# Two attention sublayers of a decoder as one row of pipeline steps with shared buffers

## The chip, the cores and the metric

The kernel runs on one core of a Trainium2 chip. The metric is device time in microseconds (us) of one launch, the median of several runs. PE is TensorE (matmuls and transposes), DVE is VectorE, ACT is ScalarE, POOL is GpSimd, SP is SyncE, which here only issues DMAs.

## The reference

A decoder of four layers, post-layernorm, over 4096 tokens (64 sequences of 64) of width 256. Each layer has self-attention, a second mixer and a feed-forward part: twelve sublayers. The tenth and eleventh are the fourth layer's two attentions, the twelfth its feed-forward part with ternary weights.

```python
def _L3_attn_ref(x, Wq, Wk, Wv, Wproj, q_rms_w, k_rms_w, subln_w):
    H, D = (16, 128)
    q = (x @ Wq).reshape(B, T, H, D)
    k = (x @ Wk).reshape(B, T, H, D)
    v = (x @ Wv).reshape(B, T, H, D)
    q = rmsnorm(q, q_rms_w)
    k = rmsnorm(k, k_rms_w)
    scores = jnp.einsum('bthd,bshd->bhts', q, k) * scale + bias[None]   # bias: ALiBi
    scores = jnp.where(causal[None, None], scores, -jnp.inf)
    attn = jax.nn.softmax(scores, axis=-1)
    y = jnp.einsum('bhts,bshd->bhtd', attn, v)
    y = rmsnorm(y, subln_w)
    y = y.transpose(0, 2, 1, 3).reshape(B, T, H * D)
    return y @ Wproj
...
def _L3_xattn_ref(hidden_states, encoder_hidden_states, attention_mask, Wq, bq, Wk, bk, Wv, bv, Wo, qn_w, kn_w):
    # NH = 16 query heads, NKV = 4 key and value heads, HD = 128
    q = (hidden_states @ Wq + bq).reshape(b, s, NH, HD).transpose(0, 2, 1, 3)
    k = (encoder_hidden_states @ Wk + bk).reshape(b, se, NKV, HD).transpose(0, 2, 1, 3)
    v = (encoder_hidden_states @ Wv + bv).reshape(b, se, NKV, HD).transpose(0, 2, 1, 3)
    k = jnp.repeat(k, GROUPS, axis=1)
    v = jnp.repeat(v, GROUPS, axis=1)
    q = _rmsnorm(q, qn_w)
    k = _rmsnorm(k, kn_w)
    scores = jnp.einsum('bhsd,bhed->bhse', q, k) * scale
    scores = scores + attention_mask[:, None, :, :]
    probs = jax.nn.softmax(scores.astype(jnp.float32), axis=-1).astype(q.dtype)
    out = jnp.einsum('bhse,bhed->bhsd', probs, v)
    out = out.transpose(0, 2, 1, 3).reshape(b, s, NH * HD)
    return out @ Wo
...
x = _layernorm(x + _L3_attn_ref(x, ...), axis=-1)
x = _layernorm(x + _L3_xattn_ref(x, ctx_2048, mask_1xSxS2_ff0, ...), axis=-1)
x = _layernorm(x + _L3_ffn_ref(x, ...), axis=-1)
```

## The kernel before

**Tiling.** The 4096 tokens are 8 groups (g) of 4 tiles (t) of 128 tokens; a tile holds two sequences. Rows live in SBUF as X[g], the encoder's rows, already transposed, as CT[g]. In both sublayers the unit of work is a step (g, t, hb), where hb is one half of the 16 heads, so 64 steps each. A step's queries are two projections of 512 columns, u=0 and u=1, four heads each. The tenth sublayer also projects two times 512 columns of keys and of values in each step. The eleventh has only four key and value heads, so one projection of k and one of v serve both steps of a tile; they are made in the step with hb=0.

**Stages.** Both sublayers are software pipelines of four stages, one pass of a Python loop per step i: projections of step i, transposes and scores of step i−1, transposes of the probabilities and the products with the values of step i−2, the output projection of step i−3. All matmuls and transposes of a stage go through PE.

**The order.** Both loops stand under a manual schedule of PE: PE runs its instructions in the order of the Python code. The other engines' instructions are placed by a scheduler. A wait between engines is a semaphore; a buffer of a pool has a tag and a number of copies (bufs), and its next user waits for the readers of the one before. PSUM has the tags p (projections, two banks), tr (transposes, two banks), s (scores, one), y (products with the values, two) and acc (output, one).

The order of PE in a step of the eleventh sublayer is: transposes of both queries of step i−1 (qT0, qT1, `heads_transposed`, lines 1643 and 275), with hb=0 of step i−1 the transposed keys (kT), then with hb=0 of step i the projections k and v, then q0 and q1 (`projected`, L1966 the addition of the bias), then at the last tile of a group the transposes of the next group's rows (xt), then the transposed probabilities of step i−2 (pt), the scores of step i−1 (L2000), the output of step i−3 (L2047) and the products with the values of step i−2 (L2030). The softmax is L2006 to L2014: times the queries' norm, plus mask, maximum, minus maximum (DVE), exponential (ACT), sum, reciprocal (DVE), times reciprocal (POOL). PSUM is left by `copy` (L254 on ACT, L256 on DVE). Norms are a sum of squares (ACT, DVE) and a power on POOL (L269). z (L2053) is the residual sum, `layernorm` (L306 its last part) turns four tiles of z into the new rows.

The order of PE in a step of the tenth: v0 v1 of step i−2, then qT0 kT0, q0, qT1 kT1, q1, the transposed y of step i−3 (yt), k0, pt of i−2, scores of i−1, k1, output of i−3, values of i−2.

**Buffers.** Each sublayer has its own pool of working tiles and its own PSUM pool. The pool of the tenth hands its tiles over one by one, the eleventh's pool as a whole: its first tiles wait until the tenth's last use is over. Weights of 1 MB come from a ring of eight buffers by SP's queue (`load`, L366); `big_weight` loads two of them. The biases of k and v and the mask are tiles of the eleventh's pool, loaded at its start. To bring the two halves of a value tile to the other half of the partitions, two small DMAs on SP's queue write vs from v (L1788 in the tenth, L1979 in the eleventh). The weight of the tenth's output projection is scaled once on ACT by the learned weight of y's norm.

**Around it.** The twelfth sublayer's ternary weights are prepared inside the eleventh (`ternary`, L2098 to L2109), some of its rows in the last 12 steps (`l3_prepare`), and its own first tiles wait for the whole of the pools before.

Of the kernel before, what the change touches and what calls it, by code (L numbers as in the profile page):

```python
# [2 lines left out]

# [6 lines left out]
F32 = mybir.dt.float32  # L10
# [4 lines left out]
ALU = mybir.AluOpType  # L15
# [12 lines left out]
LAYERS = 7  # L28
# [206 lines left out]
class Decoder:  # L235
# [154 lines left out]
    def run(self, layers):  # L390
# [12 lines left out]
        for g in (1, 2):  # L403
# [5 lines left out]
            self.l2_l3, self.l3_xattn, self.l3_ffn,  # L409
# [959 lines left out]
    def l2_l3(self, ctx):  # L1369

        shared = self.pool(ctx, "l2s", 1)
        linear = Linear(self, shared)
        for body in (self.l2_mix, self.l3_attn):
            with ExitStack() as part:
                self.psum = self.pool(part, "psum_" + body.__name__, 2, space=PSUM, reuse_waits="tile")
                body(part, linear)
# [355 lines left out]
    def l3_attn(self, ctx, linear):  # L1734


# [5 lines left out]
        wk = ctx.enter_context(self.tc.tile_pool(name="l3a", bufs=2, reuse_waits="tile"))  # L1742
        wq, wkk, wp, wv = (self.big_weight(n) for n in ("l3a_wq", "l3a_wk", "l3a_wproj", "l3a_wv"))
# [5 lines left out]
        steps = [(g, t, hb) for g in range(self.n_groups) for t in range(TG) for hb in range(2)]  # L1749
# [34 lines left out]
        def value(i, u):  # L1784
            v = projected(i, wv, u, "v", 2)
            vs = wk.tile([P, 4, P], F32, tag="vs", name="vs")
            for b in range(2):
                nc.sync.dma_start(out=vs[half(b)], in_=v[half(1 - b)])  # L1788
            state[i, "v", u] = v, vs
# [84 lines left out]
        with self.tc.manual_schedule(engines={mybir.EngineType.PE}):  # L1874
            n = len(steps)
            bank = lambda name: self.bank(name, bufs=2)
            linear.first(wk, bank)
            bias = self.distances(wk)
            for w in wp:
                nc.scalar.activation(w, w, AF.Copy, scale=sw)  # L1880
            xts[0] = wk.tile([P, 2, NTOK], F32, tag="xt", name="xt")
            ahead = []
            for i in range(n + 3):
                first, second, third, fourth = i < n, 1 <= i <= n, 2 <= i <= n + 1, i >= 3
                if first and steps[i][1:] == (0, 0):
                    if steps[i][0] + 1 < self.n_groups:
                        ahead = linear.parts(steps[i][0] + 1, wk, bank)
                    zs[steps[i][0]] = wk.tile([P, TG, D], F32, tag="z", name="z", bufs=1)
                if first and steps[i][0] == 0 and steps[i][2] == 0:
                    t = steps[i][1]  # L1890
                    ps = self.transpose4([self.X[0][:, t, c * P : (c + 1) * P] for c in range(2)], "xt")
                    self.copy(xts[0][:, :, t * P : (t + 1) * P], ps[:, :D].rearrange("p (c n) -> p c n", c=2))
                if third:
                    value(i - 2, 0)
                    value(i - 2, 1)
                if second:
                    turn(i - 1, 0)
                if first:
                    query(i, 0)
                if second:  # L1900
                    turn(i - 1, 1)
                if first:
                    query(i, 1)
                if fourth:
                    outputs_turned(i - 3)
                if first:
                    key(i, 0)
                if third:
                    turned(i - 2)
                if second:  # L1910
                    scores(i - 1)
                if first:
                    key(i, 1)
                if fourth:
                    output(i - 3)
                if third:
                    values(i - 2)
                if first:
                    g, t, hb = steps[i]
                    if ahead:  # L1920
                        ahead.pop(0)()
                        if len(ahead) == 5:
                            ahead.pop(0)()
                    if (t, hb) == (TG - 1, 0) and g + 1 < self.n_groups:
                        xts[g + 1] = self.transposed(self.X[g + 1], wk, "xt")

    def l3_xattn(self, ctx):


# [5 lines left out]
        wk = self.pool(ctx, "l3x", 2)  # L1935
        wq = self.big_weight("l3x_wq")
        kv = self.weight("l3x_wkv").rearrange("p (i c n) -> p i c n", i=2, c=2)
        self.load(kv[:, 0], ins["l3x_wk"].rearrange("(c p) n -> p c n", p=P))
        self.load(kv[:, 1], ins["l3x_wv"].rearrange("(c p) n -> p c n", p=P))
        wo = self.big_weight("l3x_wo")  # L1940
        bq = self.weight("l3x_bq")
        bk, bv = (wk.tile([P, 512], F32, tag=name, name=name, bufs=1) for name in ("l3x_bk", "l3x_bv"))
        for t, name in ((bq, "l3x_bq"), (bk, "l3x_bk"), (bv, "l3x_bv")):
            self.load(t, ins[name].broadcast_to([P, t.shape[1]]))
        qw, kw = self.column("l3x_qw"), self.column("l3x_kw")
        both = wk.tile([P, 1], F32, tag="both", name="both", bufs=1)
        nc.vector.tensor_scalar(both, kw, qw, 1.0 / math.sqrt(P), ALU.mult, ALU.mult)
        mask = wk.tile([P, S], F32, tag="mask", name="mask", bufs=1)
        for b in range(2):
            self.load(mask[b * S : (b + 1) * S], ins["mask"])  # L1950
        half = lambda b: slice(b * S, (b + 1) * S)
        steps = [(g, t, hb) for g in range(self.n_groups) for t in range(TG) for hb in range(2)]
# [16 lines left out]
        def keys_values(g, t):  # L1969
            ct = self.CT[g]  # L1970
            cs = lambda c: ct[:, c, t * P : (t + 1) * P]
            k = projected(cs, lambda c, n: kv[:, 0, c, n], slice(0, 512), bk, "k", 1)
            r = self.small(4, "hrk")
            rms(k, r, "k")
            nc.gpsimd.tensor_tensor(k, k, r.unsqueeze(2).broadcast_to([P, 4, P]), ALU.mult)
            v = projected(cs, lambda c, n: kv[:, 1, c, n], slice(0, 512), bv, "v", 2)
            vs = wk.tile([P, 4, P], F32, tag="vs", name="vs")
            for b in range(2):
                nc.sync.dma_start(out=vs[half(b)], in_=v[half(1 - b)])  # L1979
            return k, v, vs  # L1980

        def queries(g, t, hb):
            xt = xts[g]
            qs = []
            r = self.small(8, "hrq")
            for u in range(2):
                cols = slice((2 * hb + u) * 512, (2 * hb + u + 1) * 512)
                q = projected(
                    lambda c: xt[:, c, t * P : (t + 1) * P], lambda c, n: wq[c][:, n], cols, bq[:, cols], "q", 4
                )  # L1990
                rms(q, r[:, 4 * u : 4 * u + 4], "q")
                qs.append(q)
            return qs, r

        def scores(g, t, hb, qT, r):
            kT = tiles[g, t][0]
# [18 lines left out]
            return s  # L2015

        def turned(s):
            ps = self.transpose4([s[:, 2 * j : 2 * j + 2, :].rearrange("p h k -> p (h k)") for j in range(4)], "pt")
            pt = wk.tile([P, 4, P], F32, tag="pt", name="pt")
            self.copy(pt.rearrange("p j q -> p (j q)"), ps)  # L2020
            return pt

        def values(g, t, hb, pt):
            _, v, vs = tiles[g, t]
# [10 lines left out]
            for h2 in range(2):  # L2035
                yt = wk.tile([P, 4, P], F32, tag="yt", name="yt", bufs=4)
                self.copy(yt.rearrange("p j q -> p (j q)"), pss[h2])
                yts.append(yt)
            return yts

        def output(g, t, hb, yts):
# [3 lines left out]
            for h in range(8):  # L2045
                n = 8 * hb + h
                nc.tensor.matmul(  # L2047
                    acc[:, :D], yts[h % 2][:, h // 2, :], wo[n // 8][:, (n % 8) * D : (n % 8 + 1) * D],
                    start=n == 0, stop=n == 15,
                )  # L2050
            if hb == 1:
                x, z = self.X[g], zs[g]
# [3 lines left out]

        ahead = []
        with self.tc.manual_schedule(engines={mybir.EngineType.PE}):
            n = len(steps)
            xts[0] = self.transposed(self.X[0], wk, "xt")  # L2060
            for i in range(n + 3):
                if 1 <= i <= n:
                    g, t, hb = steps[i - 1]
                    qs, r = state.pop((i - 1, "q"))
                    qT = [self.heads_transposed(wk, q, "qT", bufs=4) for q in qs]
                    if hb == 0:
                        tiles[g, t][0] = self.heads_transposed(wk, tiles[g, t][0], "kT", both)
                if i < n:
                    g, t, hb = steps[i]
                    if hb == 0:  # L2070
                        tiles[g, t] = [*keys_values(g, t)]
                        if t == 0:
# [243 lines left out]
```

## Time and profile before

| | us |
|---|---|
| median of 3 runs | 4425.86 (4423.49 to 4430.15) |
| profiled execution | 4426.47 |
| its span, first to last instruction | 4424.7 |
| tenth sublayer in the span | about 1924 to 3222 |
| eleventh sublayer | about 3222 to 4124 |
| twelfth sublayer | about 4124 to 4425 |

Granted TensorE clock over the span: 0.971 of full speed. The starts of the score products (L2000) give the length of the eleventh's steps: in the even part 14.15 us from a step with hb=1 to one with hb=0, and 12.34 us from one with hb=0 to the one with hb=1. Durations in this profile that the reader will meet again: a projection of 512 columns is 1.72 us of PE, four transposes 0.44, scores 1.08, output 3.55 to 3.65, values 1.09; on DVE an operation on 128x512 numbers is 0.68 us, the next begins 0.60 us after it, or 0.72 if it needs its result; on ACT 0.58 to 0.63; on POOL a product 1.04 and a power 1.01.

A row of the timeline is to be read as: start in us of the span, duration, engine, line of the kernel, operation, written tile <- read tiles, shape, number of equal instructions, and in brackets the engine's idle time before it with what ended it.

### The profile page before, as it was taken

The page shows a single profiled execution, that of the slowest core. Times are in us where ns is not written, and L with a number is a line of the kernel's source. Part 1 is how long each engine was busy: PE and PEld are TensorE (multiplying, and loading weights), DVE is VectorE, ACT ScalarE, POOL GpSimd, SP SyncE. Part 2 cuts the span into 40 slices and gives each one's busy share as a digit, 9 for nine tenths or more (in the row PEclk, how much of TensorE's full clock was granted, in tenths as well). Part 3 has the DMA queues.
Part 4 walks back from the last instruction along what each step waited for, and adds up shares of the span by engine and source line. Part 5 has one row for each costly group of instructions (what it writes and reads, how often), then busy time and mean ns, then how long its engine had stood idle before and what let it go on. Part 6 is the DMA issues. An engine that isn't in the chain of part 4 may idle for free. (4 is left out here: it accounts for less than half of the span.)

```text
span 4424.7 us, 73910 instructions
## 1 busy us (share of the span) xinstructions
PE 4091.3 (92%) x28788; PEld 2647.7 (60%) x28808; DVE 3092.2 (70%) x6239; ACT 2022.6 (46%) x3667; POOL 1475.5 (33%) x1501
## 2 busy tenths in 40 slices
PE   8889999989888999869999999999979999999898
PEld 6645566666665555436666666666646666666566
DVE  6744548888674677877777777777667776776676
ACT  5546545666424666534444444444323322233344
POOL 4411121322421111035555555555433333333111
PEclk9989998999999999979999999999989999999999
DMA  2100012333100000111111111111310000000000
GB/s 83 65 20 10 1 39 68 84 68 75 43 2 20 1 1 1 38 34 25 30 25 30 25 29 25 30 26 29 90 30 11 10 11 11 10 11 11 8 15 17
DMA packets 99685, 128.26 MB, mean 29 GB/s; under 512 B 14916, under 2 KB 72452, under 8 KB 97928
## 3 DMA queue, kind: packets, MB, share of 16 engines
q1 hardware_dynamic: 99336, 123.53, 11.1%
q8 instruction: 228, 3.74, 0.4%
q14 instruction: 121, 0.99, 0.1%
HBM read 61.87 MB, written 19.42 MB: 18 GB/s over the span
## 5 line engine op out<-in xcount | busy, mean ns | idle before, releaser
L269 POOL TENSOR_TENSOR hrq<-hrq,neg_half 128x4 f32<-128x4 f32 x256 | 270.7, 1058 | 510.3 <-DVE hrq L267 510.2
L269 POOL TENSOR_TENSOR rstd<-rstd,neg_half 128x4 f32<-128x4 f32 (+1 forms) x171 | 149.1, 873 | 716.8 <-DVE rstd L267 642.6
L1152 DVE TENSOR_REDUCE mc<-sq 128x2 f32<-128x512 f32 x512 | 317.0, 682 | 62.4 <-PE sk L1150 62.3
L1158 ACT ACTIVATE e<-sk 128x512 f32<-128x512 f32 x512 | 265.3, 609 | 110.0 <-PE sk L1150 109.8
L269 POOL TENSOR_TENSOR hrk<-hrk,neg_half 128x4 f32<-128x4 f32 x160 | 188.2, 1176 | 289.4 <-DVE hrk L267 279.3
L1147 PE MATMUL sq<-l1x 32*128 32x256 f32 x2048 | 273.8, 405 | 2.6 <-DVE mc L1152 1.6
L1657 PE MATMUL p<-l3a_wq,xt 128*128 128x512 f32 x512 | 244.5, 601 | 11.0 <-DVE v L256 9.9
L1657 PE MATMUL p<-l3x_wq,xt 128*128 128x512 f32 x512 | 238.0, 609 | 14.0 <-DVE k L1966 13.8
L1150 PE MATMUL sk<-l1x 32*128 32x256 f32 x2048 | 250.3, 390 | 0.0
L1657 PE MATMUL p<-l3a_wk,xt 128*128 128x512 f32 x512 | 247.2, 606 | 0.0
L1147 PEld LDWEIGHTS sq<-l1x 32*128 32x128 f32 x2048 | 207.4, 193 | 56.5 <-issue 23.9
L2047 PE MATMUL acc<-l3x_wo,yt 128*128 128x256 f32 x1024 | 238.0, 386 | 0.7 <-ACT yt L254 0.7
L1657 PE MATMUL p<-l3a_wv,xt 128*128 128x512 f32 x512 | 234.3, 600 | 0.4 <-ACT y L93 0.4
L1864 PE MATMUL acc<-l3a_wproj,yt 128*128 128x256 f32 x1024 | 232.3, 380 | 0.0
L1864 PEld LDWEIGHTS acc<-l3a_wproj,yt 128*128 128x128 f32 x1024 | 194.7, 191 | 53.0 <-issue 29.2
L2047 PEld LDWEIGHTS acc<-l3x_wo,yt 128*128 128x128 f32 x1024 | 189.3, 190 | 28.2 <-ACT yt L254 0.9
L1150 PEld LDWEIGHTS sk<-l1x 32*128 32x128 f32 x2048 | 187.0, 185 | 6.6 <-issue 2.9
L1958 ACT ACTIVATE sq<-q 128x512 f32<-128x512 f32 x128 | 80.7, 630 | 206.7 <-DVE q L1966 153.5
L1657 PEld LDWEIGHTS p<-l3x_wq,xt 128*128 128x128 f32 x512 | 97.4, 196 | 126.8 <-issue 116.2
L1848 POOL TENSOR_TENSOR hry<-hry,neg_half 128x8 f32<-128x8 f32 x64 | 106.2, 1659 | 193.4 <-DVE hry L1844 193.4
L275 PEld LDWEIGHTS qT<-ident,q 128*128 128x128 f32 x1024 | 118.8, 141 | 76.6 <-issue 63.8
L1186 PE MATMUL ret<-e,vt 128*32 128x256 f32 x2048 | 140.6, 390 | 18.1 <-DVE mc L1152 17.0
(395 smaller groups left out, 10207.3 us busy)
## 6 DMA issues: line engine op xcount, KB each, us to landing
vs<-v SPq DMA_DIRECT2D x320, 128.0 KB
x<-in_x SPq DMA_DIRECT2D x8, 512.0 KB
ct<-in_ctxT SPq DMA_DIRECT2D x8, 512.0 KB
cn<-in_ctx SPq DMA_DIRECT2D x8, 512.0 KB
l1x<-in_ctx SPq DMA_DIRECT2D x128, 32.0 KB
l1x_x<-x SPq DMA_DIRECT2D x8, 512.0 KB
l1x<-l1x_x SPq DMA_DIRECT2D x128, 32.0 KB
l1x_r<-r SPq DMA_DIRECT2D x128, 32.0 KB
```

Source lines behind the costliest of these rows:

```text
L269: nc.gpsimd.tensor_tensor(out, out, self.neg_half[:, :n], ALU.pow)
L275: self.nc.tensor.transpose(ps[:, j * P : (j + 1) * P], blk, self.ident)
L1147: nc.tensor.matmul(ps[:, n, :], x_[rows, j, part], c_[rows, j, :], start=True, stop=True)
L1150: nc.tensor.matmul(ps[:, n, :], c_[rows, j, part], x_[rows, j, :], start=True, stop=True)
L1152: nc.vector.tensor_reduce(mc[new % 2][:, ra + k, 2 * j : 2 * j + 2], ps, AX.X, ALU.max, negate=True)
L1158: nc.scalar.activation(es[rb + k], ps, AF.Exp, scale=scale)
L1186: nc.tensor.matmul(ret[32 * r : 32 * r + 32, :], vt[i % 2][:, lc, 4 * r + j, :], es[r][:, lc, :], start=lc == 0, stop=lc == 1,)
L1657: self.nc.tensor.matmul(ps, lhs(c), w(c, cols), start=c == 0, stop=c == 1 and bias is None)
L1848: nc.gpsimd.tensor_tensor(r, r, self.neg_half[:, :8], ALU.pow)
L1864: nc.tensor.matmul(acc[:, :D], yts[h % 2][:, h // 2, :], wp[n // 8][:, (n % 8) * D : (n % 8 + 1) * D], start=n == 0, stop=n == 15,)
L1958: nc.scalar.activation(sq, x, AF.Square)
L2047: nc.tensor.matmul(acc[:, :D], yts[h % 2][:, h // 2, :], wo[n // 8][:, (n % 8) * D : (n % 8 + 1) * D], start=n == 0, stop=n == 15,)
```

## The change

The loops of both sublayers become one loop over a row of 131 passes: the steps of the tenth, then those of the eleventh, then three passes to drain. Each pass calls the stages of whichever sublayer the step belongs to, so in the passes around the seam early stages belong to the eleventh and late ones to the tenth. Both use the tenth's pool of working tiles and one PSUM pool. In detail:

- The eleventh's weights of k, v and q and the bias of q are loaded at the end of the tenth's last step (i = n−1), its biases of k and v one pass later into the tile that held the tenth's ALiBi bias, its output weight at i = n+1. The rows of group 0 are transposed at i = n−2.
- In the pass of the eleventh's step 0 ("turning") k, q0, q1 and v are projected at the pass's end.
- The order of PE in a step of the eleventh is now: qT0, k (hb=0), q0, qT1, q1, kT of i−1, pt of i−2, v (hb=0), output of i−3, scores of i−1, values of i−2, and xt at the end.
- Buffers: qT and kT three each (before: four and two in the eleventh), q three (four), k two (one), the eleventh's yt take the tenth's tags y and yt.
- The tenth's weights are loaded in the order q, k, v, output (before: q, k, output, v), and the two scalings of its output weight move from before the loop to the ends of steps 0 and 1.

```diff
-        for body in (self.l2_mix, self.l3_attn):
+        for body in (self.l2_mix, self.l3_attentions):
...
+    def l3_attentions(self, ctx, linear):
+        wk = ctx.enter_context(self.tc.tile_pool(name="l3a", bufs=2, reuse_waits="tile"))
+        steps = [(g, t, hb) for g in range(self.n_groups) for t in range(TG) for hb in range(2)]
+        n = len(steps)
+        none = lambda *a: None
+        with self.tc.manual_schedule(engines={mybir.EngineType.PE}):
+            one, two = self.l3_attn(wk, steps, linear), self.l3_xattn(wk, steps)
+            row = [(one, i) for i in range(n)] + [(two, i) for i in range(n)]
+            for i in range(2 * n + 3):
+                at = lambda j: row[j] if 0 <= j < len(row) else (None, j)
+
+                def do(stage, name, *a):
+                    which, j = at(i - stage)
+                    if which is not None:
+                        getattr(which, name, none)(j, *a)
+
+                turning = i == n
+                do(0, "start")
+                do(2, "value")
+                if i == n + 1:
+                    two.load_output()
+                do(1, "turn", 0)
+                if not turning:
+                    do(0, "query", 0)
+                do(1, "turn", 1)
+                if not turning:
+                    do(0, "query", 1)
+                do(3, "outputs_turned")
+                do(1, "key_turned")
+                do(0, "key", 0)
+                do(2, "turned")
+                if not turning:
+                    do(0, "late")
+                if i > n + 2:
+                    do(3, "output")
+                do(1, "scores")
+                do(0, "key", 1)
+                if i <= n + 2:
+                    do(3, "output")
+                do(2, "values")
+                if turning:
+
+                    two.load_biases()
+                    do(0, "query", 0)
+                    do(0, "query", 1)
+                    do(0, "late")
+                do(0, "end")
+                if i == n - 2:
+                    two.rows(0)
+                if i == n - 1:
+                    two.load()
...
-        wq, wkk, wp, wv = (self.big_weight(n) for n in ("l3a_wq", "l3a_wk", "l3a_wproj", "l3a_wv"))
+        wq, wkk, wv, wp = (self.big_weight(n) for n in ("l3a_wq", "l3a_wk", "l3a_wv", "l3a_wproj"))
...
+        def end(i):
+            g, t, hb = steps[i]
+            if i < len(wp):
+                nc.scalar.activation(wp[i], wp[i], AF.Copy, scale=sw)
...
-    def l3_xattn(self, ctx):
+    def l3_xattn(self, wk, steps):
...
-        wk = self.pool(ctx, "l3x", 2)
...
+        def load():
+
+            w.kv = self.weight("l3x_wkv").rearrange("p (i c n) -> p i c n", i=2, c=2)
+            self.load(w.kv[:, 0], ins["l3x_wk"].rearrange("(c p) n -> p c n", p=P))
+            self.load(w.kv[:, 1], ins["l3x_wv"].rearrange("(c p) n -> p c n", p=P))
+            w.q = self.big_weight("l3x_wq")
+            w.bq = self.weight("l3x_bq")
+            self.load(w.bq, ins["l3x_bq"].broadcast_to([P, WCOLS]))
+
+        def load_biases():
+            both_ = wk.tile([P, 2, 512], F32, tag="bias", name="biases", bufs=1)
+            w.bk, w.bv = both_[:, 0], both_[:, 1]
+            for t, name in ((w.bk, "l3x_bk"), (w.bv, "l3x_bv")):
+                self.load(t, ins[name].broadcast_to([P, 512]))
+
+        def load_output():
+            w.o = self.big_weight("l3x_wo")
...
+        def query(i, u):
+
+            g, t, hb = steps[i]
+            if u == 0:
+                state[i, "r"] = self.small(8, "hrq")
+                if hb == 0:
+                    k = projected(cs(g, t), lambda c, n: w.kv[:, 0, c, n], slice(0, 512), w.bk, "k", 2)
...
+        def late(i):
+
+            g, t, hb = steps[i]
+            if hb == 0:
+                v = projected(cs(g, t), lambda c, n: w.kv[:, 1, c, n], slice(0, 512), w.bv, "v", 2)
+                vs = wk.tile([P, 4, P], F32, tag="vs", name="vs")
...
+        def turn(i, u):
+            state[i, "T", u] = self.heads_transposed(wk, state.pop((i, "q", u)), "qT", bufs=3)
+
+        def key_turned(i):
+            g, t, hb = steps[i]
+            if hb == 0:
+                tiles[g, t, "k"] = self.heads_transposed(wk, state.pop((i, "k")), "kT", both, bufs=3)
...
-                yt = wk.tile([P, 4, P], F32, tag="yt", name="yt", bufs=4)
+                yt = wk.tile([P, 4, P], F32, tag=("y", "yt")[h2], name="yt", bufs=2)
...
+        def end(i):
+            g, t, hb = steps[i]
+            if (t, hb) == (TG - 1, 0) and g + 1 < self.n_groups:
+                rows(g + 1)
+
+            if len(steps) - i in (12, 8):
+                ahead.extend(self.l3_prepare(len(self.l3_rows)))
+            if ahead:
+                ahead.pop(0)()
```

## The prediction

> **What bounds the kernel now.** I read the page first, for who is busy over the span:
>
> ```profile
> PE 4091.3 (92%) x28788; PEld 2647.7 (60%) x28808; DVE 3092.2 (70%) x6239; ACT 2022.6 (46%) x3667; POOL 1475.5 (33%) x1501
> ```
>
> TensorE (PE) leads with 92%, but that is a mean over many stages, so I cut the two stages that change into stretches: 3200–3240 is the boundary between tenth and eleventh sublayer, 3300–4075 the even part of the eleventh. The columns are length, then busy us and count of PE, weight loads, DVE, ACT and POOL, then the granted clock, the DMA share and GB/s.
>
> ```profile
> 3200.00:3222.00 22.00, 15.88 (x95) 11.87 (x94) 8.10 (x16) 2.26 (x4) 4.08 (x4) 0.81 0.45 148
> 3222.00:3240.00 18.00, 5.44 (x9) 2.11 (x8) 7.71 (x15) 1.33 (x3) 1.45 (x2) 0.62 0.25 73
> 3300.00:4075.00 775.00, 732.05 (x5142) 498.28 (x5139) 553.62 (x1108) 233.19 (x382) 264.15 (x243) 0.99 0.05 11
> ```
>
> In the even part PE lacks 43 of 775 us, so it is the bound there. In the boundary it lacks 18.7 of 40 us and part of its clock. The view of waits for PE in 3300–4075 says what the 43 us are (seconds in all, times, longest, in us):
>
> ```profile
> PE kT L275 <- DVE qT L256: 31.1, 26, 1.8
> PE kT L275 <- POOL s L2014: 7.2, 2, 3.6
> PE pt L275 <- ACT xt L254: 3.2, 7, 0.8
> PE p L1657 <- DVE k L1966: 1.2, 1, 1.2
> PE p L1657 <- DVE v L1966: 0.2, 1, 0.2
> ```
>
> So nearly all is one wait: the transposes of k (kT) need a PSUM bank of the pair "tr" that the copy of qT has not left, because qT0, qT1 and kT stand directly one after the other. The timeline of the boundary (start, duration, engine, line, operation; in brackets the idle time before it and its releaser):
>
> ```profile
> 3212.30 2.11 PE L275 MATMUL yt<-ident,y 128*128 128x128 f32 x8 [6.12 <-POOL y L1850]
> ...
> 3230.95 0.34 SPq L366 DMA_DIRECT2D l3x_bk<-in_l3x_bk  x1
> ...
> 3234.54 0.69 DVE L1966 TENSOR_TENSOR k<-p,l3x_bk 128x512 f32<-128x512 f32 x1 [2.81 <-DMA l3x_bk<-in_l3x_bk]
> ...
> 3235.37 5.55 PE L1657 MATMUL p<-l3x_wq,xt 128*128 128x512 f32 x8 [12.56 <-DVE k L1966]
> ...
> 3245.96 1.12 PE L275 MATMUL kT<-ident,k 128*128 128x128 f32 x4 [3.41 <-POOL k L1975]
> ```
>
> The old pipeline drains (2.54 us before the yt at 3198.58, 6.12 before 3212.30). Then the bias of k, a tile of a new pool, is loaded only when the last normalisation of the tenth (3229.43 to 3230.81) has left the old pool; k, and behind it q, wait 12.56 us. Then the new pipeline fills from nothing. Lastly the softmax, of which the change shows more than before. In the timeline of the tail, where DVE is free, it is all that lies between these two rows:
>
> ```profile
> 4103.63 1.15 PE L2000 MATMUL s<-kT,qT 128*64 128x64 f32 x32
> ...
> 4110.91 0.66 PE L275 MATMUL pt<-ident,s 128*128 128x128 f32 x4 [1.39 <-POOL s L2014]
> ```
>
> 7.28 us from the first score product to the transposes of the probabilities (pt) that it feeds. In the even part pt never waits for it: the next scores come 12 to 14 us later.
>
> [...] after 3.61 us of idle at 3649.65 the q projections take 6.12 us, where they take 3.60 elsewhere; the kT waits of up to 1.8 us never do this. [...] the trace shows SP's three loads in a row from 3230.95, right behind the normalisation's end. [...]
>
> **The change part by part.** Times below come from rows of before, laid out by hand in the changed order of each engine.
>
> *Joined stages.* k, q0, q1 and v of the eleventh's step 0 now stand behind the tenth's step 62 values, at 3192.3. Their weights are issued one step earlier, near 3173, into slots that are free then; 2.5 MB at the 350 GB/s of 3170–3180 is some 7 us, so they land near 3180. The small biases take 3.6 us from issue to use in before (3230.95 to 3234.54) and are issued about 3189: 3192.9, just in time. The 6.9 us of projections cover the 2.54 us wait. The tenth's v of step 63 stays in its bank, so q1 waits about 1 us; first scores of the eleventh near 3210 (before 3251.66). Then one stall is new: v and vs of the second half of step 63 share slots with those of the first half, so the copy and the two vs loads come only after the first half of the values, and the loads stand in SP's order behind the 1 MB load of the FFN's weight, which waits for the tenth's outputs. [...] The third scores come at 3246.4, where before has them at 3272.63: −26.2 us.
>
> *Scaling of wproj and its loads at the tenth's start.* Two ACT instructions of 2.00 us (1857.03, 1861.61) move two steps later, and the wproj loads go behind wv's. DVE's chain to the next normalised rows hides them in both places: 0, at most +1.5.
>
> *Order of a step in the eleventh, 64 times.* kT moves behind the q projections: its bank is then free, and the 31.1 us of the first wait go. But output moves ahead of scores, so that scores stand at the end of the step, and their softmax must be ready at pt of the next step. A step with hb=0 (I call it A) has three projections (k, q0, q1 at 1.72 each, v comes after) between scores and pt, a step with hb=1 (B) only two plus kT. A offers 8.2 us against a softmax of 7.5 (with other work on DVE between): no stall, 14.02 us instead of 14.15. B offers 1.08+1.09+0.44+1.72+0.44+1.72+0.44 = 6.93 (scores, values, qT0, q0, qT1, q1, kT). The softmax's DVE row, 0.60 to 0.72 apart, with the y copy, a qT copy and q's bias add between, then reciprocal and POOL's 1.04, is ready at 7.89: 0.96 us of new stall. B is 11.98 instead of 12.34 us. A pair gains 0.13+0.36, rounded down to 0.43 for A's uncertainty: 16 plain pairs −6.9.
>
> *B with a layernorm, 7 groups.* z comes from output, which now ends just as scores begin. DVE then has z, statistics, the score's first step, and four normalising instructions (1.38 us, 3229.43) that wait for POOL's power (1.0), all ahead of the mask add. pt is ready at 10.33: stall 3.4 us, interval 14.42 instead of 12.88 (with A, +1.47 a pair): 7 × 1.47 = +10.3. [...] I take 1.2: +8.4.
>
> *Steps that transpose the next group's rows, 7.* xt moves to the end of the step and its bank wait covers the pt stall: A and B together 26.82 instead of 27.89: −7.5.
>
> *The FFN's weight preparation* sits in two bursts (6.0 us at 3630–3670, 4.75 at 3740–3775) and 3.25 us of row preparation near the end. They put DVE and POOL work between the softmax's, and the slack is gone: +3 each as an estimate, from 0 (same place) to +10 (twice the price).
>
> *Tail.* Last scores interval 11.6 instead of 8.43, as the softmax is fully exposed, +3.2; the rest −0.5. The FFN's first tile waits for the whole old pool in both: 0.
>
> *Smaller buffers* (q 4 to 3, qT 4 to 3; k and kT one more each): PE's order already leaves each a step: 0, with +0.3 a step (one copy's lag, 0.58 less the 0.3 to spare) if it is a wait: up to +10, held for the range.
>
> Sum: −26.2 + 3.2 − 0.5 = −23.5 for boundary and tail; −6.9 + 10.3 + 8.4 − 7.5 + 3 + 3 = +10.3 for the steps; −13.2 in all. The profiled run is 4426.47 us (span 4424.7 and 1.8 around it), 0.6 above the median: 4413.3, and by the median 4412.7. I say 4413.
>
> **The rivals.**
> *Nothing replaces the kT wait* (15 in 100). The softmax keeps up, as at A; then 31.1 + 23.5 go: 4372. For it: DVE is 71% busy in the even part, and a better placed row could end 1 us earlier. Against it: 7.28 us measured with DVE free is already over B's 6.93.
>
> *The softmax in front of pt becomes the bound* (25 in 100), the slower side. Place: pt in B steps. Price: my laid-out chain uses DVE's 0.60 spacing at independent neighbours; at 0.72 throughout it is 0.6 us longer, 16 × 0.6 = 9.6; [...] and the preparation costs 10 rather than 3 us more: +27 on −13: 4440. It decides when pt's waits with the lost clock pass 67 us in all (mine are 16 × 0.96 + 7 × 3.4 + 8.4 + 6 = 54, and 13 more eat the gain).
>
> *The boundary doesn't join as written* (5 in 100): a bias or vs load held on SP, or the FFN weight's load in front, lets PE drain again. With 20 of the 23.5 us lost: 4433. Against it: of the loads only vs and the output weight have anything late in front.
>
> **How the numbers follow.** Forecast 55 in 100, its own range 4396 to 4428 (no half clock and no preparation cost: −14 us[...]). To leave no more than 2 in 10 out, the range goes up to 4446, which takes in the slower rival and its buffers, and down to 4388; 4372 stays out. A measurement of this kernel tells 0.2%, 8.9 us. Of the forecast's 55, 40 lie beyond it, 14 within, 1 above; of the first rival all 15 are faster; of the second 23 slower, 2 within; of the third 3 within, 2 slower. Faster 55, same 19, slower 26.
>
> **What would show it.** In the waits of PE, kT <- DVE qT gone, pt <- POOL s about 1 us in some 16 B steps and 3 or more in layernorm steps; with half clock, projections of 5 to 6 us there. The interval between scores, A 14.0, B 12.0. In the boundary no bias wait and scores near 3210, but a gap of 4 to 5 us inside the values at 3220–3230. A pt wait absent in B steps, or above 2 us in plain ones, would prove the forecast wrong, as would a drained PE between 3222 and 3240.

## The result and the profile after

The changed kernel takes 4417.39 us (median of 19 runs, 4411.74 to 4422.95) against 4424.14 us for the kernel before in the same runs. The ratio is 0.9986 with a 95% interval of 0.9978 to 0.9993, a gain of 3 to 10 us. The forecast was 13. The profiled execution has a span of 4416.7 us, 8.0 less than that of before. More than half of this can't be put down to the change: at the first score products of the tenth sublayer the trace is already 4.5 us ahead, and the traces of the experiments, all with the same code for the nine sublayers ahead, stand between 5.8 us ahead of the kernel before and 0.9 us behind it at that point. Where positions in two traces are compared below, they are counted from these first score products.

TensorE's busy time is the same as before within 0.1%; what changed is where it waits. In the list of waits of TensorE over 3300–4075, the even part of the eleventh sublayer (all us, times, longest), the kernel after has:

```profile
PE pt L276 <- POOL s L2064: 33.3, 21, 3.2
PE qT L276 <- DVE xt L257: 6.9, 2, 3.5
PE qT L276 <- ACT xt L255: 4.1, 6, 0.7
PE p L1658 <- DVE k L2005: 0.5, 1, 0.5
```

The 31.1 us of kT waiting for qT's copy are gone, and 33.3 us of pt waiting for the softmax's last product stand in their place. The list over 3200–3300, with the seam in it:

```profile
PE yt L276 <- POOL y L1904: 4.6, 1, 4.6
PE y L1886 <- DMA vs<-v: 4.3, 1, 4.3
PE pt L276 <- POOL s L2064: 2.5, 2, 1.7
```

The bias wait of 12.56 us and the kT wait of 3.41 us are gone; the vs wait in the values of step 63 was foreseen, the wait for y was not. A layernorm step in the timeline:

```profile
3348.71 0.69 DVE L2056 TENSOR_TENSOR s<-s,hrq 128x512 f32<-128x512 f32 x1
3348.88 1.01 POOL L270 TENSOR_TENSOR rstd<-rstd,neg_half 128x4 f32<-128x4 f32 x1 [2.78 <-DVE rstd L268]
3349.92 1.38 DVE L307 TENSOR_SCALAR x<-z,bnmv,rstd 128x256 f32<-128x256 f32 x4 [0.52 <-POOL rstd L270]
3351.22 0.68 DVE L2057 TENSOR_TENSOR s<-s,mask 128x512 f32<-128x512 f32 x1
...
3357.71 1.12 PE L276 MATMUL pt<-ident,s 128*128 128x128 f32 x4 [3.18 <-POOL s L2064]
3358.62 4.62 PE L2101 MATMUL acc<-l3x_wo,yt 128*128 128x256 f32 x16
```

The four normalising instructions, behind POOL's power, stand between the softmax's first and second instruction; pt comes 3.18 us late and runs in 1.12 us instead of 0.60, the output in 4.62 instead of 3.62: half clock (the granted clock is 0.55 over 3357.5–3361). The tail, where both pipelines have run dry:

```profile
4086.75 0.66 PE L276 MATMUL pt<-ident,s 128*128 128x128 f32 x4 [4.28 <-POOL s L2064]
4087.24 5.30 PE L2101 MATMUL acc<-l3x_wo,yt 128*128 128x256 f32 x16
4092.48 1.15 PE L2050 MATMUL s<-kT,qT 128*64 128x64 f32 x32
4100.03 1.11 PE L276 MATMUL pt<-ident,s 128*128 128x128 f32 x4 [5.30 <-POOL s L2064]
4100.93 5.50 PE L2101 MATMUL acc<-l3x_wo,yt 128*128 128x256 f32 x16
```

Two waits of 4.28 and 5.30 us for the softmax, each with an output of 5.3 to 5.5 us behind it. The starts of the score products, subtracted from one another in both traces, give the balance. As in the prediction, A is a pass of the loop that projects for a step with hb=0, B for one with hb=1; the scores that end the interval are those of the step before, so an A interval runs from scores with hb=0 to scores with hb=1. (The section on the time before names the two directions the other way round: the 14.15 us lead to hb=1, the 12.34 to hb=0.)

| us | before | after | after, counted from the first row |
|---|---|---|---|
| first scores of the tenth, in the span | 1942.72 | 1938.18 (−4.5) | 0 |
| third scores of the eleventh, in the span | 3272.63 | 3253.00 (−19.6) | −15.1 |
| interval: plain A, plain B | 14.15, 12.34 | 13.96, 11.94 | |
| interval: B with layernorm | 12.88 | 16.05 | |
| interval: A and B around an xt | 27.88 | 26.69 | |
| 63rd scores, in the span | 4095.20 | 4079.20 (−16.0) | −11.5 |
| first transposes of the FFN, in the span | 4120.40 | 4111.81 (−8.6) | −4.1 |

So the boundary gained 15.1 us, the sixty steps behind it gave 3.6 back, the tail 7.4, the FFN 0.6. The 3.5 us that remain in this pair of traces lie within the 3 to 10 us that the medians give.

### The profile page after: what moved, and what is told of

Same layout as the page of the kernel before. It is cut to its first block, busy times and chain, and to the rows that moved or that the text cites. A ratio compares the mean times of both kernels' runs of the same rounds, so it can differ in the third digit from the quotient of the medians.

```text
span 4416.7 us, 73850 instructions
## 1 busy us (share of the span) xinstructions
PE 4088.2 (93%) x28808; PEld 2650.9 (60%) x28808; DVE 3098.4 (70%) x6239; ACT 2019.1 (46%) x3667; POOL 1462.5 (33%) x1501
## 5 line engine op out<-in xcount | busy, mean ns | idle before, releaser
L270 POOL TENSOR_TENSOR hrq<-hrq,neg_half 128x4 f32<-128x4 f32 x256 | 258.3, 1009 | 309.0 <-DVE hrq L268 298.0
L2101 PEld LDWEIGHTS acc<-l3x_wo,yt 128*128 128x128 f32 x1024 | 202.3, 200 | 42.7 <-issue 14.3
L2064 POOL TENSOR_TENSOR s<-s,smx 128x512 f32<-128x512 f32 x64 | 66.7, 1042 | 481.5 <-DVE smx L2063 241.1
L255 ACT COPY yt<-y 128x512 f32<-128x512 f32 x64 | 37.5, 586 | 383.7 <-PE y L2082 383.7
L276 PE MATMUL pt<-ident,s 128*128 128x128 f32 x768 | 117.4, 284 | 58.5 <-POOL s L2064 46.2
L276 PE MATMUL qT<-ident,q 128*128 128x128 f32 x1024 | 158.2, 277 | 12.4 <-DVE xt L257 6.9
```

The source lines that it names most:

```text
L270: nc.gpsimd.tensor_tensor(out, out, self.neg_half[:, :n], ALU.pow)
L276: self.nc.tensor.transpose(ps[:, j * P : (j + 1) * P], blk, self.ident)
L2064: nc.gpsimd.tensor_tensor(s, s, wide(sm), ALU.mult)
L2101: nc.tensor.matmul(acc[:, :D], yts[h % 2][:, h // 2, :], w.o[n // 8][:, (n % 8) * D : (n % 8 + 1) * D], start=n == 0, stop=n == 15,)
```

## The experiments

The experiments were measured in four batches, each beside runs of the kernel before; its medians in them are 4424.87, 4424.83, 4422.23 and 4421.86 us. A median is that of 4 to 21 runs.

| run | median, us | ratio to before, 95% interval |
|---|---|---|
| join_only | 4401.62 | 0.9950 (0.9938 to 0.9963) |
| reorder_only | 4433.06 | 1.0017 (1.0009 to 1.0024) |
| scores_first | 4374.46 | 0.9885 (0.9872 to 0.9899) |
| ln_act | 4394.83 | 0.9935 (0.9923 to 0.9947) |
| hold | 4419.96 | 0.9991 (0.9985 to 0.9998) |
| scores_only | 4385.90 | 0.9911 (0.9897 to 0.9924) |
| sf_hold | 4372.26 | 0.9878 (0.9864 to 0.9891) |
| sf_pieces | 4380.57 | 0.9907 (0.9892 to 0.9921) |
| sf_both | 4369.54 | 0.9881 (0.9864 to 0.9897) |
| after_ones | 4411.16 | 0.9973 (0.9964 to 0.9981) |
| sf_ones | 4349.54 | 0.9834 (0.9821 to 0.9847) |

**The two halves of the change alone.** The change joins the stages and turns the order of a step round; each was made without the other.

join_only, against the kernel after:

```diff
+                if i > n + 2:
+                    do(1, "turn", 0)
+                    do(1, "turn", 1)
+                    do(1, "key_turned")
+                    do(0, "late")
+                    do(0, "query", 0)
+                    do(0, "query", 1)
+                    do(0, "rows_turned")
+                    do(2, "turned")
+                    do(1, "scores")
+                    do(3, "output")
+                    do(2, "values")
+                    do(0, "end")
+                    continue
```

> The stages of the two sublayers joined as in the change, but in the eleventh's pure passes TensorE keeps the order of before (both qT, kT, v, k, q0, q1, xt, pt, scores, output, values). Theory (the join gains about 19.6 us at the boundary and the new order gives some 11 back, 3.6 in the steps and 7.4 in the tail): the kT waits of about 31 us return, intervals between scores are 14.15 and 12.34 us again, and the time is 4424 - 19.6 = about 4404, some 12 us faster than the change. Rival (the new order is what pays, the seam is a wash): slower than the change, 4420 or more.

reorder_only, against the kernel before, in the eleventh's loop (keys and values, and the two queries, taken apart for it; k has two buffers):

```diff
-                    qT = [self.heads_transposed(wk, q, "qT", bufs=4) for q in qs]
-                    if hb == 0:
-                        tiles[g, t][0] = self.heads_transposed(wk, tiles[g, t][0], "kT", both)
+                    qT = [self.heads_transposed(wk, qs[0], "qT", bufs=4)]
...
+                    q0 = query(g, t, hb, 0, rq)
+                if second:
+                    qT.append(self.heads_transposed(wk, qs[1], "qT", bufs=4))
+                if i < n:
+                    state[i, "q"] = [q0, query(g, t, hb, 1, rq)], rq
+                if second and steps[i - 1][2] == 0:
+                    at = tiles[steps[i - 1][:2]]
+                    at[0] = self.heads_transposed(wk, at[0], "kT", both)
...
-                if 1 <= i <= n:
-                    state[i - 1, "s"] = scores(*steps[i - 1], qT, r)
                 if i >= 3:
                     output(*steps[i - 3], state.pop((i - 3, "y")))
+                if second:
+                    state[i - 1, "s"] = scores(*steps[i - 1], qT, r)
```

> The kernel before, with separate stages and its own buffers, and only the eleventh's order within a step changed to that of the change. Theory: the 31 us of kT waits go and pt waits of some 33 us with half clock after the layernorm steps come, tail included: 4424 + 11 = about 4435. Rival (the new order is what pays): faster than before, down to 4400.

Measured: 4401.6 and 4433.1 us, one faster than the change by some 16 us, the other slower than before. In join_only the wait list over 3300–4075 has kT <- qT's copy back with 33.7 us, and the steps take 14.15 and 12.34 us. Its third scores come 19.3 us earlier than before, its 63rd 21.7 us, both counted from the tenth's first scores. In reorder_only, over 3300–4075, the first line is that of the change:

```profile
PE pt L275 <- POOL s L2013: 33.7, 21, 3.2
```

Counted from the tenth's first scores, its 63rd scores come 2.8 us behind those of the kernel before, its last 7.6 us behind them, close to the 8.2 us of the medians: the new order loses a little in the steps and the rest in the tail. The rival, that the new order pays, is out: the whole gain is the join's, and the new order gives part of it away.

**Why pt waits.** scores_first puts the scores ahead of the output again and kT ahead of q1:

```diff
                 do(1, "turn", 1)
+                if i > n + 2:
+                    do(1, "key_turned")
                 if not turning:
                     do(0, "query", 1)
                 do(3, "outputs_turned")
-                do(1, "key_turned")
+                if i <= n + 2:
+                    do(1, "key_turned")
...
-                if i > n + 2:
-                    do(3, "output")
                 do(1, "scores")
                 do(0, "key", 1)
-                if i <= n + 2:
-                    do(3, "output")
+                do(3, "output")
                 do(2, "values")
```

> The change, but in the eleventh's pure passes the scores stand ahead of the output projection, as before the change, and kT ahead of q1 instead of behind it. Theory (pt waits because the softmax has only 6.9 us of TensorE work behind the scores in steps with hb=1): 3.6 us more cover, pt waits go and kT waits don't come back; steps with hb=1 take about 11.2 us, the layernorm ones too: 16 x 0.76 + 7 x 4.9 + 7 x 0.9 + about 5 in the tail = some 55 us less than the change: about 4362. Rival (the softmax's row on VectorE is the limit wherever the scores stand, the wait only changes its name): 4405 to 4417.

Measured: 4374.5 us, 43 less than the change instead of the 55 expected. Its list of waits over 3300–4060:

```profile
PE qT L276 <- ACT xt L255: 8.3, 2, 4.2
PE qT L276 <- DVE xt L257: 4.5, 5, 0.9
PE pt L276 <- POOL s L2064: 2.0, 2, 1.4
```

pt's 33 us have shrunk to 2, and kT's did not come back. B steps take 11.16 us, those with a layernorm too (16.05 in the change). That is the number expected, and the rival, that VectorE's row is the limit anyway, is out. Two terms were too good: A steps take 14.16 instead of 13.96 us (31 × 0.2 = 6 us; no wait shows there, but the starts of the rows say where they are: from v to the product behind it 1.82 us when these are the scores and 1.72 when it is the output, from the output to the product behind it 3.65 instead of 3.55; why is open), and steps with an xt 13.14 instead of 12.73 where I had expected a gain.

ln_act leaves the order and takes the layernorm's four instructions off VectorE:

```diff
                 if t == TG - 1:
-                    self.layernorm(x, z)
+                    self.normalized(x, z)
```

> The change, but the eleventh's layernorm applies mean and deviation with four ACT instructions (and one small VectorE one) instead of four VectorE ones. Theory (in layernorm steps these four, waiting for POOL's power ahead of the softmax's mask add, make the 3.2 us wait and the half clock behind it): layernorm steps fall from 16.05 to about 12.4 us, 7 x 3.6 = 25 us: about 4392. Rival (the layernorm is not what holds the softmax there; the half clock comes from elsewhere): within 5 us of the change.

Measured: 4394.8 us, 23 less than the change. The step shown above now reads:

```profile
3348.77 0.16 DVE L326 SCALAR_TENSOR_TENSOR nmr<-bnmv,rstd 128x4 f32<-128x4 f32 x1 [0.52 <-POOL rstd L270]
3348.85 0.68 DVE L2057 TENSOR_TENSOR s<-s,mask 128x512 f32<-128x512 f32 x1
3348.96 2.08 ACT L328 ACTIVATE x<-z,nmr,rstd 128x256 f32<-128x256 f32 x4 [6.50 <-DVE nmr L326]
...
3354.74 0.66 PE L276 MATMUL pt<-ident,s 128*128 128x128 f32 x4 [1.37 <-POOL s L2064]
```

The wait is 1.37 instead of 3.18 us, pt runs in 0.66 instead of 1.12: the half clock is gone too. The step falls from 15.78 to 12.55 us.

scores_only is scores_first without kT's move:

```diff
-                if i > n + 2:
-                    do(3, "output")
                 do(1, "scores")
                 do(0, "key", 1)
-                if i <= n + 2:
-                    do(3, "output")
+                do(3, "output")
```

> The change with scores ahead of the output projection, but kT left behind q1. Theory: the pt waits go as in scores_first, but kT's copy on ACT (0.69 us and two handovers) is then covered only by pt's 0.5, so scores wait for it about 0.5 us in each of the 32 tiles: 4374 + 16 = about 4390. Rival (kT's place doesn't matter): 4374.

Measured: 4385.9 us, with this first line in its list of waits over 3300–4060:

```profile
PE s L2047 <- ACT kT L1652: 14.4, 29, 4.0
```

B steps take 11.57 us instead of 11.16. So an output between kT and scores does have a use, to cover kT's copy; with kT ahead of q1 that wait is gone, and A steps are no longer than in scores_only (14.16 us in both).

**What held up the seam.** First I blamed VectorE, which stands at the sum over the FFN's weight while its load lands (3.90 us idle ahead of that sum in the kernel after, ended by the load). hold makes that load late:

```diff
+                if i == n + 2:
+                    self.held = {name: self.fetched(name, self.X[-1][:, 0, :1]) for name in ("l3f_wfc", "l3f_wproj")}
...
+    def fetched(self, name, behind):
+        w = self.weight(name)
+        n = self.ins[name].shape[1]
+        self.nc.gpsimd.tensor_copy(w[:, :1], behind)
+        self.load(w.rearrange("p (c n) -> p c n", n=n), self.ins[name].rearrange("(c p) n -> p c n", p=P))
+        return w
```

> The change, but the loads of the FFN's two weights wait for the tenth's last normalised rows (a one-column POOL copy into the weight's tile ahead of each load), so that SP sends the last vs loads first and VectorE doesn't stand at the sum over l3f_wfc while the tenth's last y is due. Theory (the 7 us by which the boundary missed its forecast are VectorE's wait for that weight: y, then yt at half clock): second scores of the eleventh near 3229 instead of 3238.4, third near 3245 instead of 3253.0; 4 to 9 us faster in all, 4408 to 4413, as the two sums over the weights (2.3 us each) then stand in front of a softmax. Rival (y is late because of POOL or of the values themselves): the second scores stay within 2 us of 3238.

> Scores_first and hold together. Theory: the two are in different places and add up: 4374 less 4 to 9: 4365 to 4370. Rival (what the seam gains is lost again in the steps behind it, which wait for VectorE): 4374.

In hold the second scores come at 3227.23 and the third at 3241.85 us, 9.9 us before those of the change as counted above; but the next two intervals grow by 6.8 and 5.8 us, and nothing is left: 4420.0 us. In sf_hold, on top of scores_first, the third scores gain 10.1 us and the last are left with 2.8 (4372.3 us, not told apart from 4374.5). I had expected some of it back, not all. sf_pieces, on top of sf_hold, made VectorE's sums small and moved the load of the second weight eight passes later:

```diff
-        nc.vector.tensor_reduce(col, w, AX.X, ALU.add, apply_absolute_value=True)
+        cols = self.small(4, "tcols", bufs=2)
+        for i in range(4):
+            nc.vector.tensor_reduce(
+                cols[:, i : i + 1], w[:, i * 512 : (i + 1) * 512], AX.X, ALU.add, apply_absolute_value=True
+            )
+        nc.vector.tensor_reduce(col, cols, AX.X, ALU.add)
```

> Sf_hold with the sums over the two FFN weights taken apart: each is four sums of 512 columns instead of one of 2048, and the second weight's load waits for the first group's normalised rows of the eleventh, so that the two don't fall in one step. Theory (what hold gained at the seam, 9 us, was given back because two sums of 2.29 us and VectorE's order stand whole in front of a softmax): pieces fit between the softmax's dependent instructions and in the 3.6 us that scores_first left free; third scores to fourth near 15.7 us again, 4372 - 7 = about 4365. Rival (the give-back is the loads or POOL's part of the preparation): 4372.

A miss: 4380.6 us, and the profiled run, with 4374.3 us the fastest of its four, has an interval of 22.56 us for the fourth scores and one of 23.03 for the twelfth. POOL's and VectorE's rows in its timeline say why:

```profile
3248.16 0.20 DVE L2067 RECIPROCAL smx<-smx 128x8 f32<-128x8 f32 x1
```
```profile
3249.61 0.40 POOL L2157 PARTITION_ALL_REDUCE tgam<-tcol  x1 [5.75 <-PE p L1658]
3256.80 1.03 POOL L2068 TENSOR_TENSOR s<-s,smx 128x512 f32<-128x512 f32 x1 [6.79 <-issue]
```

The reciprocal that the product needs was there at 3248.4, yet POOL began it at 3256.8: 7.2 us after an all-reduce that is shown with 0.40. So it is POOL, not VectorE. The rows of sf_hold tell why sf_pieces was slower than it:

```profile
3254.81 0.78 POOL L2150 PARTITION_ALL_REDUCE tgam<-tcol  x2 [5.91 <-DVE s L2062]
3262.41 1.03 POOL L2066 TENSOR_TENSOR s<-s,smx 128x512 f32<-128x512 f32 x1 [6.83 <-issue]
```

There both all-reduces stand in a row with one gap behind them, and one interval of 23.01 us; by moving the second weight sf_pieces took the pair apart, and its twelfth scores pay a second time (23.03 us instead of 14.16). Read again, the timeline of POOL in the kernel after has the same at the seam, and that of the kernel before, too, ahead of the last layernorm of the tenth (L2099, then L269):

```profile
3221.36 0.40 POOL L2141 PARTITION_ALL_REDUCE tgam<-tcol  x1 [6.48 <-issue]
3228.89 1.68 POOL L1902 TENSOR_TENSOR hry<-hry,neg_half 128x8 f32<-128x8 f32 x1 [7.12 <-DVE hrq L1998]
```
```profile
3219.08 0.40 POOL L2099 PARTITION_ALL_REDUCE tgam<-tcol  x1 [5.83 <-issue]
3228.34 1.05 POOL L269 TENSOR_TENSOR rstd<-rstd,neg_half 128x4 f32<-128x4 f32 x1 [8.87 <-issue]
```

The power for y was ready to run at 3224.6, when VectorE had written hry. sf_both adds to sf_pieces an edit of another wait, the rows' transposes in two halves around the values:

```diff
                 do(3, "output")
+                if i > n + 2:
+                    do(0, "rows_half", 0)
                 do(2, "values")
+                if i > n + 2:
+                    do(0, "rows_half", 1)
```

> Sf_pieces, and the transposes of the next group's rows made in two halves, one ahead of the values and one behind, instead of both at the step's end. Theory (the 13.14 us of these seven steps hold 1.1 us of waiting for the bank of xt): 7 x 1.1 = some 7 us less than sf_pieces: about 4358. Rival (the wait only moves to the next transposes): no change.

4369.5 us; the xt steps fall from 13.14 to 12.03 us as expected, which makes 7.8 of the 11 us between it and sf_pieces. The last pair takes the all-reduce away, from the change alone (after_ones) and from sf_both (sf_ones), where the load's place stays as in each. Both have the sums in four pieces, as sf_both had:

```diff
-        nc.gpsimd.partition_all_reduce(gam, col, P, bass_isa.ReduceOp.add)
-        nc.vector.tensor_scalar_mul(gam, gam, 1.0 / (P * WCOLS))
...
+        ones = wk.tile([P, 4, P], F32, tag="sq", name="ones")
+        nc.vector.memset(ones[:, 0, :], 1.0 / (P * WCOLS))
+        ps = self.bank("tgam", tag="tr", bufs=2)
+        nc.tensor.matmul(ps[:, :1], ones[:, 0, :], col, start=True, stop=True)
+        nc.vector.tensor_copy(gam, ps[:, :1])
```

> The change, but the sum of each FFN weight over the partitions is a product with a matrix of ones on TensorE (one column, in the passes n+4 and n+6) instead of POOL's all-reduce, and the sum over the columns comes in four pieces. Loads and SP's order stay. Theory (a POOL all-reduce shows 0.40 us, but POOL's next instruction begins 7.2 to 7.5 us after its start; at the seam this holds the power for y, two steps later a softmax's product): y's power can start when VectorE has its sums, about 3225 instead of 3228.9; second scores near 3232 to 3234 instead of 3238.4, and the pt wait of 1.7 us at 3263 goes; 5 to 8 us less than the change: 4409 to 4412. Rival (VectorE's wait for the weight alone makes y late): second scores within 1 us of 3238, time as the change's.

> Sf_both with the same product of ones in place of POOL's all-reduce (passes n+4 and n+12). Theory: the two intervals of about 23 us that hold an all-reduce fall to about 15.7 and 14.2: 4369.5 - 7 - 9 = about 4354. Rival (the give-back comes from the VectorE sums themselves): 4369.

after_ones: 4411.2 us, its second scores 24.2 us behind the first instead of 30.8, and the pt wait near 3263 gone. The rows that show it:

```profile
3226.26 1.64 POOL L1908 TENSOR_TENSOR hry<-hry,neg_half 128x8 f32<-128x8 f32 x1 [8.14 <-DVE hry L1904]
```
```profile
3231.39 1.04 PE L276 MATMUL yt<-ident,y 128*128 128x128 f32 x8
```

The power is now released by VectorE's hry itself, and yt runs without a wait, in 1.04 us instead of the 2.12 of the change. sf_ones: 4349.5 us; the two intervals of 22.9 and 23.7 us in sf_both fall to 14.2, better than expected. It is the fastest version here, 1.66% (1.53 to 1.79) below the kernel before.

## Why the prediction was right, and where its sizes were off

The direction held, and the time lies in the range; the gain is about half of the 13 us forecast. That it is not smaller is in part luck, as two large errors had opposite signs. By its own steps:

- *Joined stages: 26.2 us forecast, 15.1 found.* First scores at 3207.6, which is 3212.1 when the 4.5 us are taken out (forecast 3210), the wait for vs in the values 4.30 + 0.70 us (its signs named a gap of 4 to 5): near enough. That a load waiting in SP's order delays the vs loads was not shown: they are issued at 3213.65, right behind the copy of v (3213.04 + 0.58). From the first scores to the third it took 45.4 us instead of 36.4. What was left out is the y of step 63, then yt at half clock (granted 0.50 over 3232.7–3236). VectorE waits 1.94 us for the all-reduce's result, and POOL starts the power 4.3 us after it could. Both rows of that all-reduce were in the trace of before; the prediction puts nothing for it. after_ones regains 6.65 us in this very interval, hold 9.85; in hold the wait for vs is also shorter, 2.5 us (2.48 in sf_hold); there the FFN's 1 MB load, in the change issued at 3212.41, no longer stands in front of the vs loads. Of the signs named beforehand against the forecast, a drained TensorE between 3222 and 3240, this is a part: it lacks 4.65 of these 18 us.
- *Order of a step.* Plain steps 13.96 and 11.94 us (forecast 14.02 and 11.98), the kT wait gone, the pt wait in its place at 0.76 us (forecast 0.96). Steps with xt 26.69 a pair (26.82). The mechanism is shown by scores_first and scores_only.
- *Layernorm steps.* Wait 3.18 us (3.4); step 16.05 us (14.42 and 1.2 for a lower clock). All seven together cost 20 us (forecast 18.7). That these four instructions are the cause is shown by ln_act. The waits of 3.18 us were followed by products at half clock in all seven steps of this trace, but not in every trace: 6 of 7 in reorder_only, 5 of 7 in after_ones, 18 of 21 in these three. The forecast's 1.2 us a step, +8.4 in its sum, was an estimate of mine; the trace of before shows no such figure. A step that escaped, in after_ones, took 14.37 us:

```profile
3355.50 0.66 PE L276 MATMUL pt<-ident,s 128*128 128x128 f32 x4 [3.18 <-POOL s L2070]
3355.99 3.62 PE L2107 MATMUL acc<-l3x_wo,yt 128*128 128x256 f32 x16
```

- *The FFN's weight preparation: +6 forecast, about −1 found* (the pairs at its two bursts and in the last twelve steps against the plain ones). In the list of waits two of kT for the softmax's last product (7.2 us) give way to two of qT for the copy of xt (6.9 us); I took a price where there was an exchange.
- *Tail: +2.7 forecast, +7.4 found.* The exposed softmax was there (interval 13.28 us, forecast 11.6), but I had put in no lower clock there: outputs of 5.30 and 5.50 us instead of 3.6 to 3.7 behind waits of 4.3 and 5.3 us (granted 0.53 over 4087.5–4091 and over 4101–4105).
- *Smaller buffers and the scaling of wproj:* no wait names them; nothing, as forecast.

Three terms were mis-sized: the seam by +11.1 us, the preparation by −7 and the tail by +4.7; the second hides more than half of the first. Of the rivals, "nothing replaces the kT wait" fell at once with the 33.3 us in the list of waits. "The softmax in front of pt becomes the bound" named the right mechanism: it ate the new order's gain, and by reorder_only more than that, but not the join's. "The boundary doesn't join as written" came true in part, 11 of 26 us, by POOL's all-reduce and not by a held load.

Open stays why A steps are 0.2 us longer with the scores ahead of the output. Three buffers for v and vs, which might take the vs wait away by themselves, were not tried.

## What to carry to other kernels

When a wait is removed by moving an instruction, look for the result that the next stage needs first, and count the work that now stands between its producer and its user: here one transposition's place (kT) and the place of the scores decide some 43 us, while the wait that was removed was 31. Make such edits one at a time: the join was worth more than the whole change. And price an instruction by when its engine starts the next one, not by the duration that its row shows (POOL's all-reduce here: 7.2 to 7.6 us against 0.40).

## What the runs showed of the hardware

POOL's all-reduce over partitions is shown with 0.40 us, and in the kernel after VectorE reads its result 0.44 us after its start (3221.36, 3221.80). But in all seven places where the rows of before, after, sf_pieces and sf_hold show it, POOL's next row of another kind begins 7.19 us or more after its start; where that one was known to be ready it was 7.2 (sf_pieces, 3249.61 to 3256.80) and 7.5 (after, 3221.36 to 3228.89). Ahead of it, too, POOL's row before had ended at least 5.75 us earlier in all seven; in the trace of before its input had been there for the whole of that gap (written at 3212.5, POOL free at 3213.3, the all-reduce at 3219.08). Two in a row, as in sf_hold, share these gaps (5.91 us ahead, the next row 7.60 after the start of the first). In after_ones a product with a matrix of ones on TensorE does the same sum (0.38 us for its rows).

Waits of TensorE of 3.18 us were followed by half-speed products in 18 of 21 layernorm steps of after, reorder_only and after_ones (granted clock 0.55 over 3357.5–3361 in after), at a price of 1.4 to 1.7 us (15.78 to 16.06 us against 14.37). Single waits of up to 1.8 us, such as those of kT in the trace of before, were not (1.81 us at 3376.38, then 3.60 us for the q projections as elsewhere). Two short ones close together can be: in after_ones, waits of 0.67 and 0.94 us with one small product between them were followed by four q products in 2.81 us instead of 1.88 (3295.32), and the step took 15.74 us instead of 12.73.
